# Flamingo block, batch 16: all issue offsets redone, q of the next batch between the score steps, values and sums apart, the last batch transposed by TensorE

## The chip, the cores and the metric

The kernel runs on 1 core of one Trainium2 chip. The metric is the device time of one execution in microseconds (us). A core has a matrix engine (TensorE, PE in the profile), VectorE (DVE), ScalarE (ACT), GpSimd (POOL) and a queue engine that issues DMAs (SyncE, SP). ACT and POOL can issue DMAs too. Each engine takes its own instructions strictly in order and waits on semaphores for the others.

## What is computed

Sixteen batches of x (512 rows of 512) pass a gated cross attention to 120 context rows of 384, and then a gated linear layer with int8 weights, whose input is quantised row by row. Reduced to what matters:

```python
q = split_heads(layernorm(x) @ Wq + bq)          # 16 heads of 32
k = split_heads(ctx @ Wk + bk)                   # 120 keys
v = split_heads(ctx @ Wv + bv)
out = softmax(q @ k.T / sqrt(32)) @ v
x = x + tanh(g_xattn) * (merge_heads(out) @ Wo + bo)
h = layernorm(x)
h_scale = max(absmax(h, row), 1e-6) / 127
h_q = round(h / h_scale)                         # int8
x = x + tanh(g_ffn) * ((h_q @ weight_q.T) * h_scale * weight_scale + bias)
```

## The kernel before

Work is done batch by batch. Each batch has five plans of small steps: A (first layer norm, split of x into a high and a low fp16 half, transposes), K (keys and values), Q (queries), D (scores, exps, values, division) and W (output projection, residual, second layer norm, quantisation, linear layer, store). A product of two fp32 matrices is made of three fp16 products (high by high, high by low, low by high), which is why q takes 12 matmuls for each of its four blocks.

There is no scheduler at run time. Each step is given to `at`, which looks up an offset in the table ORDER: by the step's name and arguments, and by which batch it is (the first four and the last two have a value of their own, the ten in the middle share one). The offset is added to 43.0 times the batch's number, all steps are sorted by that sum, and issued in that order. The offsets set only the order in which each engine gets its instructions; the time follows from the waits. Steps of up to four batches are in flight: in the middle of the run the loads of batch b+3, the layer norm of b+2, the q of b+1 and the scores of b lie between each other.

The steps that the text speaks of, with the engine and the line of the profile:

- `consts`, `mx`, `mxy`, `statq`, `scaleq` (the set-up S): maxima of the weights and of the context, from which powers of two for scaling (`s_q` among them) are made; lines 660 to 850. `w_q` is split only when `s_q` is known (L740 ACT, L747 DVE).
- A: `stats` (DVE, L981), `norm` and `high` (ACT, L997, L1004), `low` (POOL, L1009), `addb` (L1012, a DMA that POOL issues and that adds the row `bob` to x), `tr` (two DMA transposes by SP, L1022, into `xT`). In batch 0 TensorE transposes instead: `tp` (L1028) and `te` (ACT or DVE).
- K: `ld` and `tr` (SP, L1062 and L1074, into the single buffer `yT`), `kproj` (PE `pk`, 36 matmuls, L1098), `vproj` (PE `pvv`, 9, L1126).
- Q: `proj(j)` (PE `pq`, 12 matmuls of 128x512, L1158) for the four blocks j, `high` (ACT, L1168) and `low` (DVE `ql`, L1173); `mx(j)` (PE `pm`, 16 small matmuls on 32 rows each, L1182) and `red` (DVE, two maxima of 1.15 us, L1189); then `mh` (ACT, L1193), `mt` (PE `pmt`, L1200), `me` (ACT, L1204). `pmt` comes once a batch and marks its beginning here.
- D: `sc(j)` (PE `pss`, 16 matmuls on 32 rows, L1232), two `ex` (ACT, L1238), `av(j)` (values, PE `od<-P,V`, L1246) and `den(j)` (sums of the exps, PE `od<-P,sel`, L1253), both on 32 columns of the array, `ev` (ACT, L1261), `rec` (DVE, L1266), `shuf` (DVE, L1272), `mul` (POOL, L1277), `high` (ACT, L1282), `low` (POOL, L1285). In the last batch each is done in two halves of the columns.
- W: `wo` (PE `pw`, 48 matmuls, L1321), `res` (DVE, L1327), `st2`, `neg`, `cen`, `mxa` (the second layer norm and the row maxima), `addb` (L1351, a DMA by POOL that adds `fbb`; in the last batch `addf`, POOL, L1354), `scal1` to `scal3`, `quant` and `integ` (ACT, in the last batch DVE, L1382), `tr` (DMA transpose by SP into `xqT`, L1390), `ffn` (PE `pf`, 16 matmuls, L1398), `deq` (DVE `t`, L1403), `fin` (POOL, L1410, in the last batch DVE), `store` (SP, L1419), and in the last batch `warm` (PE, L1415).

Buffers that tie the steps: the scores and `pm` share two buffers of two banks (`ps_s`); `pq`, `pk`, `pvv`, `pmt` and `pf` share two buffers of one bank (`ps_g`); values, sums and `pw` share one buffer of two banks (`ps_o`, tile `od`; in the last batch `pw` uses `ps_s`); x has four buffers, so the load of a batch waits for the store of the one four before.

Of the kernel before, what the change touches and what calls it, by code (L numbers as in the profile page):

```python
# [36 lines left out]
        (): 20.285,  # L37
    },
    "S.constf": {
        (): -61.498,  # L40
    },
    "S.consts": {
        (): -65.108,
    },
    "S.consts1": {
        (): -64.857,
    },
    "S.consts2": {
        (): -34.332,
    },  # L50
    "S.consts3": {
        (): -26.254,
    },
    "S.copyb": {
        (): -60.711,
    },
    "S.down": {
        ('q',): -36.441,
        ('k',): -21.893,
        ('v',): -8.99,  # L60
    },
    "S.gate": {
        (): -3.985,
    },
    "S.gated": {
        ('bo', 0): 2.913,
        ('ws', 1): 0.661,
        ('fb', 1): 25.539,
    },
    "S.hi": {  # L70
        ('q', 0): -33.832,
        ('q', 1): -34.046,
        ('k', 0): -16.961,
        ('k', 1): -12.421,
        ('v', 0): -3.664,
        ('v', 1): -3.521,
        ('o', 0): -2.556,
        ('o', 1): 4.164,
    },
    "S.ld": {  # L80
        ('q', 0): -200.327,
        ('q', 1): -222.024,
        ('k', 0): -39.801,
        ('k', 1): -51.704,
        ('v', 0): -17.89,
        ('v', 1): -65.179,
    },
    "S.ldb": {
        (0,): -227.564,
        (1,): -210.907,  # L90
        (2,): -196.824,
    },
    "S.ldf": {
        (): -13.35,
    },
    "S.ldg": {
        (0,): -110.502,
        (1,): -17.854,
    },
    "S.ldo": {  # L100
        (0,): -56.994,
        (1,): -110.753,
    },
    "S.ldrow": {
        ('bv',): -32.795,
        ('bo',): -20.106,
        ('fb',): -109.216,
        ('ws',): -66.859,
    },
    "S.ldy": {  # L110
        (0,): -111.074,
        (1,): -200.113,
        (2,): -113.255,
        (3,): -67.61,
        (4,): -111.682,
        (5,): -111.646,
    },
    "S.lo": {
        ('q', 0): -33.546,
        ('q', 1): -33.653,  # L120
        ('k', 0): -11.456,
        ('k', 1): -11.206,
        ('v', 0): -2.02,
        ('v', 1): 1.162,
        ('o', 0): 24.181,
        ('o', 1): 23.573,
    },
    "S.mx": {
        ('q', 0): -195.144,
        ('q', 1): -191.105,  # L130
        ('k', 0): -33.438,
        ('k', 1): -26.29,
        ('v', 0): -16.889,
        ('v', 1): -18.355,
        ('o', 0): -19.212,
        ('o', 1): -23.931,
    },
    "S.mxy": {
        (0,): -33.367,
        (1,): -53.098,  # L140
        (2,): -33.403,
        (3,): -26.325,
        (4,): -31.401,
        (5,): -34.475,
    },
    "S.scalek": {
        (): -20.142,
    },
    "S.scalek2": {
        (): -19.177,  # L150
    },
    "S.scaleq": {
        (): -35.369,
    },
    "S.scalev": {
        (): -6.38,
    },
    "S.scalev2": {
        (): 3.092,
    },  # L160
    "S.scl_w": {
        ('v', 0): -5.773,
        ('v', 1): -5.165,
        ('o', 0): -3.771,
        ('o', 1): -3.592,
        ('k', 0): -19.963,
        ('k', 1): -12.707,
    },
    "S.spread": {
        ('q',): -36.227,  # L170
        ('k',): -21.607,
        ('v',): -6.881,
    },
    "S.statk": {
        (): -25.468,
    },
    "S.statq": {
        (): -58.209,
    },
    "S.statv": {  # L180
        (): -14.816,
    },
    "S.top": {
        ('q',): -45.163,
        ('k',): -22.858,
        ('v',): -10.92,
    },
    "S.trf": {
        (): 50.739,
    },  # L190
    "S.turnb": {
        (): -61.104,
    },
    "S.up": {
        ('q',): -46.128,
        ('k',): -23.895,
        ('v',): -12.6,
    },
    "S.warm": {
        (0,): -49.559,  # L200
        (1,): -28.506,
        (2,): -20.428,
        (3,): -35.19,
        (4,): -7.631,
        (5,): -43.983,
        (6,): -46.378,
        (7,): -36.405,
    },
    "load_x": {
        (): (-230.531, -172.483, -57.423, -63.392, -61.247, -83.98, -103.532),  # L210
    },
    "A.addb": {
        (): (16.961, 0.697, 2.556, -13.815, -39.944, -32.402, -15.602),
    },
    "A.high": {
        (0,): (-45.627, -67.038, -41.981, -38.764, -42.625, -39.408, -66.394),
        (1,): (-51.596, -71.041, -37.513, -38.693, -37.978, -50.31, -47.093),
        (2,): (-51.525, -71.077, -39.372, -38.729, -37.942, -50.202, -47.45),
        (3,): (-54.17, -66.43, -40.23, -38.657, -37.906, -38.228, -48.701),
    },  # L220
    "A.low": {
        (0,): (-41.445, -61.283, -40.552, -37.621, -30.257, -35.404, -52.311),
        (1,): (-48.844, -70.183, -32.152, -35.154, -37.656, -42.589, -44.162),
        (2,): (-40.266, -70.684, -37.263, -37.192, -37.335, -39.05, -30.079),
        (3,): (-50.167, -60.926, -39.086, -33.153, -31.115, -35.869, -31.33),
    },
    "A.norm": {
        (0,): (-60.747, -70.934, -43.518, -46.485, -43.447, -58.888, -67.86),
        (1,): (-51.632, -73.829, -42.053, -45.413, -43.876, -52.419, -60.246),
        (2,): (-59.925, -73.758, -41.731, -47.307, -44.555, -58.995, -48.558),  # L230
        (3,): (-55.957, -67.467, -41.052, -47.271, -43.375, -60.497, -66.609),
    },
    "A.scal1": {
        (): (-62.248, -76.617, -44.734, -55.85, -46.092, -70.576, -75.438),
    },
    "A.scal2": {
        (): (-61.069, -76.51, -44.591, -49.952, -45.448, -68.789, -74.901),
    },
    "A.stats": {
        (0,): (-207.118, -80.835, -52.883, -58.567, -49.202, -78.69, -75.902),  # L240
        (1,): (-204.259, -79.155, -52.562, -58.495, -53.741, -78.941, -86.697),
        (2,): (-203.651, -80.585, -52.74, -58.173, -56.636, -78.762, -80.478),
        (3,): (-204.009, -79.191, -54.063, -58.352, -55.385, -78.905, -83.123),
    },
    "A.te": {
        (0, 0): (-30.936, None, None, None, None, None, None),
        (0, 1): (-34.725, None, None, None, None, None, None),
        (0, 2): (-33.796, None, None, None, None, None, None),
        (0, 3): (-34.261, None, None, None, None, None, None),
        (1, 0): (-33.867, None, None, None, None, None, None),  # L250
        (1, 1): (-35.047, None, None, None, None, None, None),
        (1, 2): (-30.901, None, None, None, None, None, None),
        (1, 3): (-36.691, None, None, None, None, None, None),
    },
    "A.tp": {
        (0, 0): (-33.939, None, None, None, None, None, None),
        (0, 1): (-39.3, None, None, None, None, None, None),
        (0, 2): (-34.082, None, None, None, None, None, None),
        (0, 3): (-35.44, None, None, None, None, None, None),
        (1, 0): (-34.153, None, None, None, None, None, None),  # L260
        (1, 1): (-35.798, None, None, None, None, None, None),
        (1, 2): (-34.01, None, None, None, None, None, None),
        (1, 3): (-36.727, None, None, None, None, None, None),
    },
    "A.tr": {
        (0,): (None, -60.783, -28.399, -25.039, -25.754, -30.293, -21.75),
        (1,): (None, -56.601, -25.11, -32.044, -27.469, -31.866, -20.07),
    },
    "D.av": {
        (0, 0): (7.167, 6.702, 13.386, 9.025, -1.984, -0.161, 3.521),  # L270
        (1, 0): (8.775, 8.418, 16.782, 13.493, -1.233, 3.557, 6.881),
        (2, 0): (14.566, 9.776, 24.002, 14.744, 0.34, 20.07, 20.463),
        (3, 0): (20.642, 13.064, 26.147, 15.888, 5.558, 24.574, 25.897),
# [1222 lines left out]
```

## Time and profile before

| | us |
|---|---|
| median of 3 runs | 758.23 (757.19 to 759.46) |
| the profiled execution | 756.32 |
| its span, from the first to the last instruction | 754.5 |
| first `pmt` (batch 0) | 63.10 |
| last `pmt` (batch 15) | 695.47 |
| a batch from `pmt` to `pmt`, eight times in the middle | 42.73 |

In a profile, times of instructions are durations on the engine; matmuls overlap, so the time from the start of one to the start of the next tells more than a duration. A bracket after an instruction gives the idle time of its engine before it and what ended it. Rows with an x and a number merge that many instructions. The busy shares are PE 95%, DVE 75%, ACT 67% and POOL 60%; the clock granted to TensorE is full but for the very end.

### The profile page before, as it was taken

To read this page: it belongs to the slowest core of one execution; us is meant where nothing else is said; L and a number is where in the kernel's file an instruction comes from. 1 tells how busy PE (TensorE), PEld (TensorE's weight loads), DVE (VectorE), ACT (ScalarE), POOL (GpSimd) and SP (SyncE) were. 2 spreads that over 40 slices of the span, in tenths; PEclk is the share of its full clock that TensorE was granted. 3 is DMA by queue.
4 is the path that set the end of the run, shared out by engine and by line. 5 is a ranking of instruction groups with operands and counts; after the bars stand their busy time and mean duration, and the time that the engine had idled before them with its cause. 6 is when DMAs were issued, how large, how long until landed. Compare 5 with 4: busy or idle time off the path is not lost. (4 is left out here: it accounts for less than half of the span.)

```text
span 754.5 us, 15917 instructions
## 1 busy us (share of the span) xinstructions
PE 714.1 (95%) x6442; PEld 320.8 (43%) x6442; DVE 563.8 (75%) x1130; ACT 509.3 (67%) x742; POOL 450.0 (60%) x569
## 2 busy tenths in 40 slices
PE   4889899999999999999999999999999899999994
PEld 2344444444444444444444444444444344444441
DVE  5976767588686877869596877869596876768685
ACT  3657686675857686685858587685858566666850
POOL 5423856565765676656575776656565763665374
PEclk9999999999999999999999999999999999999997
DMA  9652575475897587784949688694949668565064
GB/s 346 186 142 77 96 115 102 89 193 93 191 135 169 107 172 157 99 211 76 210 73 199 120 148 180 96 205 76 207 85 177 152 113 195 93 144 84 2 139 140
DMA packets 137625, 105.55 MB, mean 140 GB/s; under 512 B 111691, under 2 KB 114135, under 8 KB 133583
## 3 DMA queue, kind: packets, MB, share of 16 engines
q1 hardware_dynamic: 120767, 71.24, 39.5%
q0 software_dynamic: 16368, 32.51, 25.8%
q8 instruction: 50, 0.82, 0.4%
q10 hardware_dynamic: 416, 0.79, 0.3%
q14 instruction: 24, 0.20, 0.1%
HBM read 27.65 MB, written 16.78 MB: 59 GB/s over the span
## 5 line engine op out<-in xcount | busy, mean ns | idle before, releaser
L1158 PE MATMUL pq<-xT,w_q 128*128 128x512 f16 x768 | 175.9, 382 | 6.3 <-DVE ql L1173 2.5
L1321 PE MATMUL pw<-w_o,ohl 128*128 128x512 f16 x768 | 176.7, 379 | 2.6 <-DVE x L1327 1.4
L1189 DVE TENSOR_REDUCE M<-pm 128x8 f32<-128x960 f32 x128 | 142.9, 1149 | 17.5 <-PE pm L1182 16.4
L1238 ACT ACTIVATE P<-pss,e_s 120x1024 f32<-120x1024 f32 (+1 forms) x136 | 137.4, 1061 | 25.0 <-PE pss L1232 24.5
L1158 PEld LDWEIGHTS <-w_q 128*128 128x128 f16 x768 | 72.5, 98 | 97.7 <-issue 12.7
L1321 PEld LDWEIGHTS <-ohl 128*128 128x128 f16 x768 | 72.2, 98 | 91.3 <-issue 6.7
L1009 POOL TENSOR_TENSOR xl<-xf,xh 128x512 f16<-128x512 f32 x64 | 77.2, 1280 | 55.3 <-ACT xh L1004 55.3
L1277 POOL TENSOR_TENSOR ou<-ou,R 128x512 f32<-128x512 f32 x60 | 75.5, 1270 | 50.8 <-DVE R L1272 50.1
L1410 POOL TENSOR_TENSOR x<-t,x 128x512 f32<-128x512 f32 x60 | 76.1, 1280 | 15.1 <-DVE t L1403 7.9
L1285 POOL TENSOR_TENSOR ohl<-ou,ohl 128x512 f16<-128x512 f32 (+1 forms) x68 | 73.5, 1099 | 10.9 <-ACT ohl L1282 10.9
L1403 DVE SCALAR_TENSOR_TENSOR t<-pf,xs,wsb 128x512 f32<-128x512 f32 x64 | 47.3, 741 | 42.2 <-PE pf L1398 40.9
L997 ACT ACTIVATE xf<-x,m,r 128x512 f32<-128x512 f32 x62 | 47.1, 802 | 45.8 <-DVE m L991 45.8
L1246 PE MATMUL od<-P,V 120*32 120x512 f32 (+1 forms) x544 | 69.0, 579 | 2.6 <-DVE x L1327 1.2
L1398 PE MATMUL pf<-w_f,xqT 128*128 128x512 f16 x256 | 67.1, 389 | 3.5 <-DMA xqT<-xq 3.5
L1253 PE MATMUL od<-P,sel 120*32 120x256 f32 (+1 forms) x1088 | 70.2, 371 | 0.0
L1168 ACT ACTIVATE qh<-pq,bq 128x512 f16<-128x512 f32 x64 | 43.7, 683 | 34.0 <-PE pq L1158 33.5
L1261 ACT ACTIVATE ou<-od,s_o 128x512 f32<-128x512 f32 (+1 forms) x68 | 45.1, 663 | 26.7 <-DVE rc L1266 14.4
L1282 ACT ACTIVATE ohl<-ou 128x512 f16<-128x512 f32 (+1 forms) x68 | 39.7, 600 | 31.6 <-POOL ou L1277 30.6
L660 DVE TENSOR_REDUCE am<-xc 128x1 f32<-128x512 f32 x64 | 42.1, 675 | 24.1 <-ACT xc L1345 24.1
L1253 PEld LDWEIGHTS od<-P,sel 120*32 120x32 f32 x1088 | 40.6, 109 | 44.5 <-issue 37.1
L1327 DVE SCALAR_TENSOR_TENSOR x<-pw,c_o,x 128x1024 f32<-128x1024 f32 (+1 forms) x34 | 41.3, 1217 | 23.9 <-PE pw L1321 23.9
L1173 DVE SCALAR_TENSOR_TENSOR ql<-pq,bq,qh 128x512 f16<-128x512 f32 x64 | 47.4, 740 | 12.3 <-ACT qh L1168 12.3
(151 smaller groups left out, 1049.7 us busy)
## 6 DMA issues: line engine op xcount, KB each, us to landing
x<-in_x_dram SPq DMA_DIRECT2D x16, 1024.0 KB, 5.1
x<-bob POOLq DMA_DIRECT2D x16, 1024.0 KB, 8.8
x<-fbb POOLq DMA_DIRECT2D x15, 1024.0 KB, 8.6
out_dram<-x SPq DMA_DIRECT2D x15, 1024.0 KB, 3.9
ys<-in_ctx_dram SPq DMA_DIRECT2D x6, 480.0 KB, 6.9
yt<-in_ctx_dram SPq DMA_DIRECT2D x16, 180.0 KB, 4.4
wfq<-in_L_xattn_Wq_dram SPq DMA_DIRECT2D x2, 512.0 KB, 5.9
wfo<-in_L_xattn_Wo_dram SPq DMA_DIRECT2D x2, 512.0 KB, 6.4
```

The lines of the kernel that those rows point to most:

```text
L1009: pool.tensor_tensor(box["xl"][:, s, :], box["xf", s], box["xh"][:, s, :], ALU.subtract)
L1158: pe.matmul(pq.rearrange("p (s t) -> p s t", t=128), w_q[:, wi, c, 128 * j : 128 * j + 128], xT[b, xi][:, c], start=n == 0, stop=n == 3 * ...
L1173: dve.scalar_tensor_tensor(QL[b][:, j, :], box["p", j], bq4[:, j : j + 1], QH[b][:, j, :], ALU.add, ALU.subtract)
L1189: dve.tensor_reduce(box["M"][:, 2 * h : 2 * h + 2, :, j], pm, AX.X, ALU.max)
L1238: act.activation(P[j, h, c], box["s", j, c][h][0:KV], AF.Exp, scale=e_s[0:KV])
L1246: pe.matmul(box["o", c][r], V[b][:, 128 * j + 32 * g : 128 * j + 32 * g + 32], P[j, g // 2, c][:, g % 2, :], start=True, stop=True, tile_p ...
L1253: pe.matmul(box["den", c][r, 0 : wd // 2], sel[:, h, j, :], P[j, g // 2, c][:, g % 2, wd // 2 * h : wd // 2 * (h + 1)], start=j == 0 and h ...
L1277: eng.tensor_tensor(u, u, box["R", g, c], ALU.mult)
L1285: pool.tensor_tensor(OT[b][:, 1, g, cols[c]], box["u", g][:, cols[c]], OT[b][:, 0, g, cols[c]], ALU.subtract)
L1321: pe.matmul(box["w", p][:, k, :], OT[b][:, oi, g, 128 * s : 128 * s + 128], w_o[:, wi, g, :], start=g == 0 and n == 0, stop=g == NG - 1 an ...
L1398: pe.matmul(pf.rearrange("p (o n) -> p o n", n=128), box["T"][:, s * CQ + c, :], w_fv[:, c], start=c == 0, stop=c == CQ - 1)
L1410: eng.tensor_tensor(x1, box["t", s], x1, ALU.add)
```

## The change

All values of ORDER are new. In the middle batches this does the following to the lists of the engines. On PE, q of the next batch, which stood in one piece after the last sums, begins before the last score step; 24 of the 48 `pw` of a batch go between the first and the second score step; `pk` follows the second score step; the sums of the third and fourth group go together, ahead of the values of those groups; `pf` goes to the end of the batch, just before `pmt`. On SP the store stands between the two transposes of x. In the set-up, all loads and maxima have another order; before the first `pmt` PE has one block of q of batch 1, where it had all four.

Beside ORDER three places change: two of the four `addf` of the last batch go to DVE; the odd `fin` of the batch before the last go to DVE; and the last batch's quantised rows are transposed by TensorE, with a copy by ACT, instead of by DMA. The core of the diff:

```diff
 ORDER = {
...
     "D.av": {
-        (0, 0): (7.167, 6.702, 13.386, 9.025, -1.984, -0.161, 3.521),
-        (1, 0): (8.775, 8.418, 16.782, 13.493, -1.233, 3.557, 6.881),
-        (2, 0): (14.566, 9.776, 24.002, 14.744, 0.34, 20.07, 20.463),
-        (3, 0): (20.642, 13.064, 26.147, 15.888, 5.558, 24.574, 25.897),
+        (0, 0): (1.782, -2.024, 0.467, 4.134, -1.574, 1.228, 2.024),
+        (1, 0): (3.096, 0.294, 5.691, 8.216, -0.778, 10.638, 7.317),
+        (2, 0): (19.424, 5.379, 13.509, 12.54, 1.193, 18.179, 10.741),
+        (3, 0): (25.34, 7.628, 22.019, 22.226, 2.508, 25.409, 23.922),
...
     "D.den": {
-        (0, 0): (7.172, 6.707, 13.391, 9.03, -1.979, -0.156, 3.526),
-        (1, 0): (8.78, 8.423, 16.787, 13.498, -1.228, 3.562, 6.886),
-        (2, 0): (14.571, 9.781, 24.007, 14.749, 0.345, 20.075, 20.468),
-        (3, 0): (20.647, 13.069, 26.152, 15.893, 5.563, 24.579, 25.902),
+        (0, 0): (1.816, -1.193, 0.502, 4.549, -1.228, 5.241, 2.473),
+        (1, 0): (2.992, 0.986, 6.659, 7.939, -0.917, 11.433, 7.109),
+        (2, 0): (17.21, 5.656, 13.232, 8.147, 0.225, 14.893, 10.015),
+        (3, 0): (19.217, 6.556, 13.301, 12.298, 2.439, 16.449, 16.968),
...
     "Q.proj": {
-        (0,): (-28.363, -55.814, -14.78, -23.752, -24.431, -28.22, -17.139),
-        (1,): (-24.109, -47.915, -13.1, -16.532, -24.145, -26.397, -16.818),
-        (2,): (-25.36, -46.7, -10.205, -12.635, -22.215, -21.107, -14.709),
-        (3,): (-20.821, -43.554, -5.451, -16.174, -17.568, -21.679, -12.493),
+        (0,): (-31.601, -42.291, -35.165, -37.655, -39.143, -61.317, -43.329),
+        (1,): (-10.638, -48.518, -24.302, -28.765, -36.79, -34.922, -35.787),
+        (2,): (-15.481, -37.932, -23.16, -22.261, -18.733, -34.611, -18.767),
+        (3,): (-9.323, -35.095, -18.525, -20.67, -29.56, -30.667, -23.922),
...
         def addf(s):
-            pool.tensor_tensor(xt[b][:, s, :], xt[b][:, s, :], fbb, ALU.add)
+            (pool if s < 2 else dve).tensor_tensor(xt[b][:, s, :], xt[b][:, s, :], fbb, ALU.add)
...
+        def trp(s):
+            if box.get("T") is None:
+                box["T"] = hp.tile([128, NS * CQ, 128], HP, tag="xqT", name="xqT")
+            box["tp", s] = pt = ps_s.tile([128, 2, 512], FP, tag="s", name="ptq")[:, 0, :]
+            for c in range(CQ):
+                pe.matmul(pt[:, 128 * c : 128 * c + 128], box["q"][:, s, 128 * c : 128 * c + 128], ident,
+                          start=True, stop=True)
+
+        def tre(s):
+            dst = box["T"][:, CQ * s : CQ * s + CQ, :].rearrange("d c p -> d (c p)")
+            act.activation(dst, box["tp", s], AF.Copy)
...
         def fin(s):
             x1 = xt[b][:, s, :]
-            eng = dve if last else pool
+            eng = dve if last or b == B - 2 and s % 2 else pool
             eng.tensor_tensor(x1, box["t", s], x1, ALU.add)
...
         if last:
             for s in range(NS):
                 at(2 * z + 48.5 + s, addf, s)
+                at(2 * z + 52.2 + 0.6 * s, trp, s)
+                at(2 * z + 52.5 + 0.6 * s, tre, s)
         else:
             at(2 * z + 48.5, addb)
...
-            at(2 * z + 52.2 + 0.6 * k, tr, k)
+            if not last:
+                at(2 * z + 52.2 + 0.6 * k, tr, k)
```

The seven values of a row are for batch 0, batch 1, the middle ones (4 to 13), batch 14, batch 15, batch 2 and batch 3. The first number that a call hands to `at` is not used; the offset comes from ORDER.

## The prediction

> **What bounds the kernel now.** The page's first part comes first, then TensorE's timeline over one batch.
>
> ```profile
> PE 714.1 (95%) x6442; PEld 320.8 (43%) x6442; DVE 563.8 (75%) x1130; ACT 509.3 (67%) x742; POOL 450.0 (60%) x569
> ```
>
> TensorE is the only engine near full, so an in-order engine that hardly waits sets the time. A batch period runs from one transposed-maxima step `pmt` (L1200) to the next:
>
> ```profile
> 395.45 0.40 PE L1200 MATMUL pmt<-ident,Mh 128*128 128x128 f16 x4
> 397.76 2.06 PE L1098 MATMUL pk<-yT,w_k 128*128 128x120 f16 x36
> 399.76 0.67 PE L1232 MATMUL pss<-qh,KHP 32*128 32x512 f16 x4
> ...
> 401.01 1.04 PE L1398 MATMUL pf<-w_f,xqT 128*128 128x512 f16 x4
> 401.97 1.07 PE L1246 MATMUL od<-P,V 120*32 120x512 f32 x8
> 402.86 1.08 PE L1253 MATMUL od<-P,sel 120*32 120x256 f32 x16
> 403.87 0.39 PE L1232 MATMUL pss<-qh,KHP 32*128 32x512 f16 x4
> ...
> 423.19 2.76 PE L1321 MATMUL pw<-w_o,ohl 128*128 128x512 f16 x12
> 425.79 2.75 PE L1158 MATMUL pq<-xT,w_q 128*128 128x512 f16 x12
> 428.38 2.75 PE L1321 MATMUL pw<-w_o,ohl 128*128 128x512 f16 x12
> 431.06 0.39 PE L1182 MATMUL pm<-KHP,qh 32*128 32x120 f16 x16
> 431.38 1.04 PE L1398 MATMUL pf<-w_f,xqT 128*128 128x512 f16 x4
> 432.50 2.75 PE L1321 MATMUL pw<-w_o,ohl 128*128 128x512 f16 x12
> ...
> 438.18 0.40 PE L1200 MATMUL pmt<-ident,Mh 128*128 128x128 f16 x4
> ```
>
> Read starts, not durations, which overlap. The period is 438.18 - 395.45 = 42.73. Twelve wide matmuls take 425.79 - 423.19 = 2.60, so 0.2165 each; before `pm` they take 2.68. `od<-P,V` takes 0.89, `od<-P,sel`, with the same work, 1.01. So each change between full, row-tiled and column-tiled matmuls costs 0.08 to 0.15. Two waits hide inside the durations: the second score step lasts 401.01 - 399.76 = 1.25 where the others last 0.98 (it waits for two exps of 1.06), and `pf` at 431.38 takes 1.12 for 0.87 (the next `pw` waits for the residual add). That is 0.27 + 0.25 = 0.52 a batch.
>
> The two ends are less tight. The start (timeline), then the end (windows, DVE and SP timelines):
>
> ```profile
> 40.83 1.02 PE L1158 MATMUL pq<-xT,w_q 128*128 128x512 f16 x4 [1.69 <-DMA xT<-xh]
> 43.18 3.56 PE L1158 MATMUL pq<-xT,w_q 128*128 128x512 f16 x8 [1.33 <-DMA xT<-xl]
> 63.10 0.38 PE L1200 MATMUL pmt<-ident,Mh 128*128 128x128 f16 x4 [0.98 <-DVE ql L1173]
> ```
>
> ```profile
> 738.20 2.61 SPq L1390 DMA_TRANSPOSE xqT<-xq  x2
> 742.70 4.45 PE L1398 MATMUL pf<-w_f,xqT 128*128 128x512 f16 x12 [0.15 <-DMA xqT<-xq]
> 747.93 2.49 DVE L1410 TENSOR_TENSOR x<-t,x 128x512 f32<-128x512 f32 x4
> ```
>
> The reader is to see q of batch 1 queued behind DMA transposes, and at the end a DMA transpose, then matmuls at 0.37 each, then DVE.
>
> **Sum by stages.** I priced TensorE's list of both programs by these spacings, with 0.09 to 0.15 per change of shape. Everything comes to 688.7 before and 688.3 after: the change moves work and removes none. The span of 754.5 is that work plus 65.8 of waits; only they can shrink.
>
> *Start to the first pmt.* Before: 38.8 of work, 63.1 of time, so 24.3 of waits. After, 36 of batch 1's q matmuls (7.8) stand behind this point: 31.0 of work. The q weights are ready later (DVE's list puts statistics of batch 1 and five maxima of 1.14 ahead of s_q: about 29 by the durations, 20.7 before), but `pk` no longer queues behind transposes. I keep 24.3: 55.3. Bounds: all of the later s_q shows (+8), or the two transpose waits and half the delay of `pk` go (-5).
>
> *First period.* Before 31.87 with 24.3 of work, 7.5 of waits (2.6 of them `pk` waiting for `yT`). After, 31.7 of work with q blocks between score steps, where the gaps were. Half the waits remain: 35.5; bounds 32.5 to 39.2.
>
> *Next three.* Before 129.6 with 126.0 of work; after 122.8 of work; the same waits: 126.4; bounds 124 to 130.
>
> *Eight steady periods.* After's batch is pmt, pf4, score 0, pw24, score 1, pk, values 0, sums 0, score 2, values 1, sums 1, pq12, score 3, pvv, sums 2 and 3, values 2, pm, pq24, pm, values 3, pq12, pm, pw12, pf8, pm, pf4, pw12. It has 20 changes of shape for 21 (-0.10). Both waits go: score 1 stands 5.2 behind score 0 (two exps need 2.1), score 2 4.9 behind score 1, and the second `pw` has pmt, pf4 and score 0 (2.3) for a residual add of 1.2. So 42.73 - 0.62 = 42.1. Cover by DVE rows, from pmt = 0: maxima (1.07 each) of block 2 end at -4.7, of block 3 at -1.0, `Mh` at -0.7; pmt needs it at 0. The first block's maxima end at 28.3, and `pm` of the next block needs their buffer at 29.4: 1.1 of cover. Cover that is gone costs one for one in each batch. On SP the store (3.9) now stands between `xT<-xh`, issued 1.7 past pmt, and `xT<-xl`, which lands 5.3 after its issue: between 10.6 and 17.7, read by pq12 at 16.2. I take the early end, as no accumulate runs then; the far end costs 1.5 a batch. Eight periods: 336.8; bounds 336 to 341.8 (no gain).
>
> *Sums apart from values.* Sums 3 end at 22.8 and values 3 at 30.7, so the reciprocal (1.76) and shuffles (0.35 each) run beneath pq24, and POOL multiplies three groups (1.27) and takes two lows (1.10) before the last values come; the last low ends at 37.2, its `pw` starts at 39.3. What is late next: values 3 needs `ev` of group 2, which waits for the reciprocal (as ACT does in before's waits, 14.4 in 11 times); it is there by 25.7.
>
> [...]
>
> *Last three periods.* Before 129.1 with 122.0 of work; after 125.3 plus 1.1 of the small losses that the steady period keeps and 1.6 of waits: 128; bounds 126 to 132.
>
> *Tail from the last pmt.* Before 59.0: 32.9 to the last `pw`, 22.0 to DVE's last add, 4.1 to the end. After, three `pf` leave the score steps, which then go by ACT at about 1.9 each (701.53 to 703.25 is 1.7): 34. Then SP's transposes, 738.20 to landing at 742.7, are replaced by 16 matmuls of 128 columns (four take 0.38 in the `pmt` row, 0.1 each) and four ACT copies (0.60, L1036). DVE becomes the bound: residual 0.75, statistics 0.87, four `xq` 2.5, two maxima 1.3, eight `t` of 0.74, scalars 0.75, and, taken over from POOL (1.28 there, 0.6 here), two odd adds of batch 14 and two addf, with four last adds 4.8: 16.9. With 0.25 of start and 4.1: 55.2; bounds 52 (DVE done earlier with batch 14's four `t`) to 59.
>
> Row first: matmuls of the last ten us ran at a granted clock of 0.67, 0.37 each. The sum takes the last 16 `pf` at 0.22, as DVE is behind them anyway; at the row's 0.37 they cost 2.4 more, inside the bounds above. [...]
>
> Sum: 55.3 + 35.5 + 126.4 + 336.8 + 128 + 55.2 = 737.2, where the span was 754.5. The profiled execution took 756.3, 1.8 more than its span, and the median of the runs is 1.9 above that: 737.2 + 3.7 = 741.
>
> **Rivals.** *Reorder without effect:* the work is equal (688.3), so if each stage keeps its waits, the total is 754 + 3.7 = 758. Against it: the two steady waits have visible causes. Half of it, the late s_q and no gain in the first period (+8, +4), gives 753.
>
> *Slower: transposes under POOL's accumulating DMA.* Before, SP's `xT<-xh` issue takes 6.6 to 6.84, ending as the bob accumulate (8.8) does:
>
> ```profile
> xT<-xh SPq DMA_TRANSPOSE x15, 8.2
> x<-bob POOLq DMA_DIRECT2D x16, 1024.0 KB, 8.8
> ```
>
> After, bob is issued some 20.6 past pmt, and on SP `yT`, held until `pvv` ends at 21.1, and `xqT` stand in its way. Bob ends at 29.4, `xqT` is issued then and lands 4.3 later, 33.7; `pf8` wants it at 36.3. The point is a bob of 11.4: the largest row is 12.6, and fbb, issued 7.6 before it, reaches 16.8. At 12.6 the loss is 1.2 a batch, 13 over eleven: 754; at 13.0 it is above before; at 14.5, 3.1 a batch, 775. For it: the two accumulates overlap by a microsecond. Against it: medians 8.6 and 8.8.
>
> *More than forecast:* the start's waits shrink too: 730.
>
> **How the numbers follow.** Forecast (733 to 749) 0.63; more 0.08; half the gain lost (749 to 755.9) 0.13; without effect 0.05; slower 0.11. A measurement of this kernel tells 0.3% (2.3 us) from no change: faster 0.84, same 0.05, slower 0.11. The range leaves out the tail beyond 757 and most of "more".
>
> **What would show it.** Right: pmt to pmt 42.1 in the middle; first pmt near 55; no DMA transpose before the last `pf`; DVE without gaps after the last `pw`. Wrong: TensorE waiting for `xqT` or `M` in every batch (second rival, or my 1.1 of cover), a first pmt above 60, or the last matmuls at 0.37 on the path.

## The result, and the profile after

The changed kernel took 760.9 us (median of 13 runs, 759.62 to 764.24), the kernel before 758.36 beside it (13 runs, 754.56 to 760.68). The ratio is 1.0039, with a 95% interval of 1.0023 to 1.0055: slower by 0.4%, where 741 us and a gain were forecast. The profiled execution of the changed kernel took 759.62, its span is 757.8. These are the busy times and the granted clock in 40 slices on its page:

```profile
PE 708.1 (93%) x6458; PEld 321.8 (42%) x6458; DVE 569.2 (75%) x1134; ACT 508.9 (67%) x746; POOL 450.5 (59%) x565
PEclk7699999999989999999999999999999999999999
```

TensorE still is the only engine near full, but its share has fallen. The steps from one `pmt` to the next tell where (us, from the timeline of TensorE; the stretch from the last `pmt` to the end is called the tail below):

| stretch | before | forecast | after |
|---|---|---|---|
| start to the first `pmt` | 63.1 | 55.3 | 64.5 |
| first period | 31.9 | 35.5 | 35.1 |
| next three | 129.6 | 126.4 | 135.2 (46.63, 38.81, 49.71) |
| eight steady | 341.8 | 336.8 | 334.8 (41.84 each, one 41.95) |
| last three | 129.1 | 128 | 126.0 |
| last `pmt` to the end | 59.0 | 55.2 | 62.3 |

The middle won more than forecast. Its rows in the timeline of the changed kernel (start, duration, engine, line, operation):

```profile
402.15 0.39 PE L1212 MATMUL pmt<-ident,Mh 128*128 128x128 f16 x4
402.37 1.03 PE L1423 MATMUL pf<-w_f,xqT 128*128 128x512 f16 x4
...
404.30 5.35 PE L1333 MATMUL pw<-w_o,ohl 128*128 128x512 f16 x24
409.59 0.39 PE L1244 MATMUL pss<-qh,KHP 32*128 32x512 f16 x4
...
410.56 2.06 PE L1110 MATMUL pk<-yT,w_k 128*128 128x120 f16 x36
...
440.52 1.04 PE L1423 MATMUL pf<-w_f,xqT 128*128 128x512 f16 x4
441.40 2.75 PE L1333 MATMUL pw<-w_o,ohl 128*128 128x512 f16 x12
443.99 0.39 PE L1212 MATMUL pmt<-ident,Mh 128*128 128x128 f16 x4
```

The reader is to see 443.99 - 402.15 = 41.84; score step 1 in 410.56 - 409.59 = 0.97 behind 5.3 us of `pw`, where it took 1.25; `pf` to the next `pw` in 0.88, where it took 1.12; and `pmt` to `pf` in 0.22. In the kernel before, where `pmt` began at 395.45, that last step took 0.37 (this row stands between the first two that the prediction shows):

```profile
395.82 1.04 PE L1398 MATMUL pf<-w_f,xqT 128*128 128x512 f16 x4
```

Before the first `pmt` and at the end the timeline of the changed kernel shows

```profile
38.50 2.75 PE L1170 MATMUL pq<-xT,w_q 128*128 128x512 f16 x12
...
64.47 0.38 PE L1212 MATMUL pmt<-ident,Mh 128*128 128x128 f16 x4 [1.76 <-DVE V L1145]
...
726.80 9.24 PE L1333 MATMUL pw<-w_o,ohl 128*128 128x512 f16 x42
...
747.35 3.82 PE L1423 MATMUL pf<-w_f,xqT 128*128 128x512 f16 x16
```

The first q matmul comes 14 us later than in the kernel before, the first `pmt` only 1.4 later. The last `pw` ends at 736.0, which is 40.5 after the last `pmt` (33.1 before), and from there to the end it is 21.8 (25.95 before). So the losses against the forecast lie in three places: the start (9.2), one period, that of batch 3 (49.71), and the score steps of the last batch (6.5).

### The profile page after: what moved, and what is told of

It reads as the page before. It is cut to its first block, busy times and chain, and to the rows that moved or that the text cites. A ratio compares the mean times of both kernels' runs of the same rounds, so it can differ in the third digit from the quotient of the medians.

```text
span 757.8 us, 15977 instructions
## 1 busy us (share of the span) xinstructions
PE 708.1 (93%) x6458; PEld 321.8 (42%) x6458; DVE 569.2 (75%) x1134; ACT 508.9 (67%) x746; POOL 450.5 (59%) x565
## 4 chain that ended last, share of the span: by engine, by line
PE 83%; DVE 6%; DMA 4%; ACT 4%; POOL 1%; issue 1%; SPq 0%; DVEq 0%; ACTq 0%; POOLq 0%
PE pw L1333 22%; PE pq L1170 20%; PE od L1265 8%; PE pss L1244 8%; PE od L1258 7%; PE pf L1423 7%; PE pk L1110 4%; PE pvv L1138 4%; PE pm L1194 2%; DMA x<-in_x_dram 2%; ACT P L1250 2%; DMA ys<-in_ctx_dram 1%; DMA wsb<-_L_ffn_weight_scale_dram 1%; DVE part L672 1%; POOL ou L1289 1%
## 5 line engine op out<-in xcount | busy, mean ns | idle before, releaser
L1021 POOL TENSOR_TENSOR xl<-xf,xh 128x512 f16<-128x512 f32 x64 | 75.0, 1178 | 22.8 <-ACT xh L1016 15.2
L1435 POOL TENSOR_TENSOR x<-t,x 128x512 f32<-128x512 f32 x58 | 74.0, 1288 | 18.6 <-DVE t L1428 18.4
L1339 DVE SCALAR_TENSOR_TENSOR x<-pw,c_o,x 128x1024 f32<-128x1024 f32 (+1 forms) x34 | 41.5, 1220 | 57.6 <-PE pw L1333 57.5
L1273 ACT ACTIVATE ou<-od,s_o 128x512 f32<-128x512 f32 (+1 forms) x68 | 44.9, 660 | 45.1 <-PE od L1265 18.1
L1357 ACT ACTIVATE xc<-x,nm 128x512 f32<-128x512 f32 x64 | 45.3, 716 | 29.2 <-POOL nm L1352 29.1
L1423 PE MATMUL pf<-w_f,xqT 128*128 128x512 f16 x256 | 63.2, 379 | 1.6 <-DVE t L1428 1.5
L1388 ACT ACTIVATE xc<-xc,magic,qs 128x512 f32<-128x512 f32 x64 | 50.2, 808 | 8.2 <-DVE qs L1380 8.2
L1265 PEld LDWEIGHTS od<-P,sel 120*32 120x32 f32 x1088 | 38.0, 111 | 41.3 <-issue 22.9
L1352 POOL TENSOR_SCALAR nm<-mv 128x2 f32<-128x2 f32 (+1 forms) x34 | 7.7, 225 | 77.4 <-DVE mv L1348 77.4
```

The costliest lines, as they stand in the source:

```text
L1021: pool.tensor_tensor(box["xl"][:, s, :], box["xf", s], box["xh"][:, s, :], ALU.subtract)
L1265: pe.matmul(box["den", c][r, 0 : wd // 2], sel[:, h, j, :], P[j, g // 2, c][:, g % 2, wd // 2 * h : wd // 2 * (h + 1)], start=j == 0 and h ...
L1423: pe.matmul(pf.rearrange("p (o n) -> p o n", n=128), box["T"][:, s * CQ + c, :], w_fv[:, c], start=c == 0, stop=c == CQ - 1)
L1435: eng.tensor_tensor(x1, box["t", s], x1, ALU.add)
```

## The experiments

Each ratio is to the kernel before in the same comparison; spans, periods and tails are those of the one profiled execution. Later experiments build on earlier ones, and the texts that were recorded ahead of them speak of them by number; the numbers stand in the headings and ahead of those texts.

### Batch 3: one pair of steps exchanged (experiment 1)

```
     "D.den": {
-        (2, 0): (17.21, 5.656, 13.232, 8.147, 0.225, 14.893, 10.015),
+        (2, 0): (17.21, 5.656, 13.232, 8.147, 0.225, 14.893, 10.086),
```

> One number of the changed kernel differs: in batch 3 the sums of group 2 (line 1265) are recorded just after the eviction of group 1 (line 1273) instead of just before it. No engine's list of instructions changes; only who waits for whom. Theory (values and sums lie in one PSUM tile, and what touches a tile is ordered as a whole, so this eviction waits for the sums although it reads only the values): ACT's wait of 6.26 us at 201.7 goes, the exps of the last score step come at about 205 instead of 211, and the period that took 49.71 us, which holds 4.8 of waits behind it and some 2.5 of matmuls at a lower clock, falls to 42.5 to 44; span about 751, 0.8% to 1.0% under the changed kernel. Rival (the period is long because the exps or the low part of k come late by themselves, from POOL or DVE): the period stays above 47 and the span within 2 us of 757.8.

Measured: 753.03 us, ratio 0.9968 (0.9950 to 0.9985), span 749.3; the period of batch 3 is 42.86, the other periods are unchanged, and the tail is 60.8 (62.3 in the changed kernel). ACT's timeline in the changed kernel:

```profile
199.60 2.11 ACT L1250 ACTIVATE P<-pss,e_s 120x1024 f32<-120x1024 f32 x2
207.97 0.69 ACT L1273 ACTIVATE ou<-od,s_o 128x512 f32<-128x512 f32 x1 [6.26 <-PE od L1265]
...
211.02 2.11 ACT L1250 ACTIVATE P<-pss,e_s 120x1024 f32<-120x1024 f32 x2
```

and in the experiment:

```profile
199.51 2.11 ACT L1250 ACTIVATE P<-pss,e_s 120x1024 f32<-120x1024 f32 x2
201.50 0.70 ACT L1273 ACTIVATE ou<-od,s_o 128x512 f32<-128x512 f32 x1
...
205.52 2.10 ACT L1250 ACTIVATE P<-pss,e_s 120x1024 f32<-120x1024 f32 x2
```

The eviction (L1273) needs values that were there at 201.1. It waited for the sums of the next group, which TensorE had behind q, a score step and `pvv`, and the exps of that score step stood behind it on ACT. With every engine's list unchanged, 6.85 us come back in that period.

### The last batch: sums behind their values (experiment 2)

```
-        (0, 0): (1.816, -1.193, 0.502, 4.549, -1.228, 5.241, 2.473),
-        (1, 0): (2.992, 0.986, 6.659, 7.939, -0.917, 11.433, 7.109),
...
+        (0, 0): (1.816, -1.193, 0.502, 4.549, -1.569, 5.241, 2.473),
+        (1, 0): (2.992, 0.986, 6.659, 7.939, -0.773, 11.433, 7.109),
...
```

> In the last batch alone every step of sums stands directly behind its step of values, as in the kernel before (for the last group the values are pulled ahead to the sums). Theory (the same tie of one tile: each eviction waits for the next group's sums, so that ACT's round trip is paid in every score step, and TensorE's waits then cost it its clock at 716 to 721): from the last pmt to the end of the last pw 34 to 36 us instead of 40.5, the tail 56 to 58 instead of 62.3, span 752 to 753. Rival (ACT sets these steps with 1.27 of exps, 0.47 of eviction and the four centrings, whatever the order): the stretch stays at 39 or more and the span within 2 us of 757.8.

Measured: 755.99 us, ratio 0.9993 (0.9974 to 1.0011), span 754.2. From the last `pmt` to the end of the last `pw` it is 34.8, the tail 56.7, as the theory had it; 1.7 of the gain went in the first period of this execution, where the first q block took 4.45 instead of 2.76. The time is that of the kernel before. From the last `pmt` to the last `pw` the granted clock was 1.00 (0.92 in the changed kernel). That the waits had cost the changed kernel its clock is not shown: in the last batch of the first experiment TensorE waited longer for evictions (3.8 and 1.8 us, against 2.6 and 1.8 in the changed kernel), with score rows of four at 0.11.

### The set-up in the old order (experiment 3)

The steps ahead of the first score step were sorted as in the kernel before, q of batch 1 apart; no code changed.

> The steps that the changed kernel records ahead of the first score step stand in the order of the kernel before; q of batch 1 stays between the score steps, and the statistics of batch 2, two of its normalisations and the load of batch 3 stand just behind or just ahead of the first score step. Theory (the first pmt is late since VectorE's list puts maxima that wait for loads ahead of the second normalised tile, the bias copy and s_q): s_q at about 20.7 instead of 31.5, first q matmul at about 24.5 instead of 38.5, first pmt at 56 to 59 instead of 64.5; span 750 to 753 if the first period keeps its 35. Rival (k's weights, v's chain and the eight maxima of the first batch set the first pmt, whatever stands ahead): first pmt at 62 or later, span within 2 us of 757.8, or what is won comes back in the first period.

Measured: 767.52 us, ratio 1.0158 (1.0122 to 1.0193), span 765.3. The first q matmul came at 24.26, as expected, and the first `pmt` at 66.46, later than in the changed kernel; the first period took 40.39. My edit had a fault of its own: I had put the load of batch 2 ahead of the transposes of batch 1, whose issue then took SP 8.9 us, so that `yt` of batch 1 was late and VectorE waited 5.69 for its high part ahead of k's bias. The granted clock, too, was only 0.55 to 0.76 between 40 and 66 us (1.00 from 40 to 60 in the changed kernel): `pk` took 3.78 (2.06 there), `pvv` 3.96 (2.10) and a q block 4.45 (2.76). So this run does not isolate the order; it shows that 14 us won on the first q matmul left no trace in the first `pmt`.

### The three together, and the first two (experiments 4 and 5)

Experiment 4:

> The three edits together. Theory: the three losses lie in different stretches and add up, so the span falls by 6.5 + 5.5 + 6.5 to about 739 and the time to about 742, which is what the prediction gave. Rivals: one of the stretches is paid back in the next (span 744 or more), or none of the three causes holds (span within 4 us of 757.8).

Measured: 754.28 us, ratio 0.9969 (0.9951 to 0.9988), span 753.1, not the 739 expected. The spans of the three do add up, but the start's part is a loss of 7.5, not a gain.

Experiment 5:

> The edits of the first two experiments together, the start as the change left it. Theory (two separate losses behind the tied tile): span 757.8 - 6.9 - 5.6 = 745 give or take the 2 us that the clock of the first 100 us moved between the runs so far, time about 749, 0.8% to 1.1% under the kernel before. Rival (the shorter tail and the shorter period share something): span above 748.

Measured: 748.54 us, ratio 0.9892 (0.9862 to 0.9922), span 746.6: the losses of batch 3 and of the tail are separate, and without them the change is faster than the kernel before.

### What the q work ahead of the first `pmt` cost (experiment 8)

In the kernel before, three q blocks of batch 1 with their evictions and low parts go behind score steps 0, 1 and 2 of batch 0. Other offsets shift with them, but nothing else changes its place in the list of an engine.

> The kernel before with one move: three of the four q blocks of batch 1 (36 wide matmuls, 7.8 us of work), their evictions and their low parts go from the stretch ahead of the first pmt to behind the first three score steps. The prediction's step (work taken away ahead of the first pmt shortens that stretch one for one): first pmt at 55 to 57 instead of 63.1, and the first period 3 to 5 longer. Rival (that work filled time in which TensorE would wait for k's weights and for the eight maxima of batch 0 on VectorE, which take 9 us and start at 51): first pmt at 59 to 62, and the first period 5 to 8 longer, so the span rises by 2 to 5.

Measured: 761.07 us, ratio 1.0060 (1.0035 to 1.0085), span 761.1. The first `pmt` comes at 62.32 instead of 63.10, the first period takes 38.72 instead of 31.87. The two largest waits of TensorE between 36 and 63 us in this experiment (in total, times, longest):

```profile
PE pm L1182 <- DVE M L1189: 4.2, 4, 1.3
PE pst L792 <- DVE stat L828: 3.2, 1, 3.2
```

and `pvv`, 2.12 in the kernel before, took 4.09 here, at a clock of 0.50. Of 7.8 us of work taken away 0.8 showed; the waits grew in its place, and the first period became 6.85 longer. The slower `pvv` had a part in this: `Mh`, which `pmt` needs, was there at 60.97, so with `pvv` at its 2.12 an estimated 2.1 at the most might have shown (63.10 - 60.97). Either way the prediction's step, at one for one, is refuted.

### The last batch by DMA transposes again (experiment 7)

```
-                at(2 * z + 52.2 + 0.6 * s, trp, s)
-                at(2 * z + 52.5 + 0.6 * s, tre, s)
...
-            if not last:
-                at(2 * z + 52.2 + 0.6 * k, tr, k)
+            at(2 * z + 52.2 + 0.6 * k, tr, k)
```

The two DMA transposes also get earlier offsets for the last batch.

> The fifth experiment with the last batch transposed by two DMA transposes in the places of the second and third group of TensorE's transposes, as in the kernel before. Theory (the transposes' part of the change is worth what the stretch from the last pw to the end says, 25.95 before and 21.8 after): span 3 to 5 above the fifth experiment. Rival (VectorE sets the end anyway): within 1 us of it.

Measured: 749.66 us, ratio 0.9904 (0.9869 to 0.9938), span 747.9; the tail 57.6 instead of 56.7. The transposes by TensorE are worth about 0.9, near the rival and far from the theory's 3 to 5: the last `pf` and VectorE's last add begin 0.5 later, VectorE's list behind the `pf` is the same, and the rest lies behind the last add.

### The adds back on POOL (experiment 10)

```
-            (pool if s < 2 else dve).tensor_tensor(xt[b][:, s, :], xt[b][:, s, :], fbb, ALU.add)
+            pool.tensor_tensor(xt[b][:, s, :], xt[b][:, s, :], fbb, ALU.add)
...
-            eng = dve if last or b == B - 2 and s % 2 else pool
+            eng = dve if last else pool
```

> The fifth experiment with the two odd last adds of batch 14 and the two adds of the bias of batch 15 back on POOL, as in the kernel before (0.68 and 0.6 to 1.0 each on VectorE, 1.28 to 1.5 on POOL). Theory (VectorE sets the end, as its list has no gap over 0.4 us in the last 20 us, and POOL is idle for 3.5 of them): last add 1 to 2.5 us earlier, span 744 to 745.5 against 746.6, with the same start. Rival (the end goes by the last pf matmuls, or POOL's slower adds take the place): within 0.5 of it or later.

Measured: 750.37 us, ratio 0.9913 (0.9878 to 0.9947), span 750.2, the tail 59.5 instead of 56.7. My theory fell: giving VectorE less to do made it later, by 2.8. VectorE's timeline

```profile
732.38 1.30 DVE L1394 TENSOR_SCALAR xq<-xc 128x512 f16<-128x512 f32 x1
733.60 1.22 DVE L1376 TENSOR_TENSOR a<-am,r 128x2 f32<-128x2 f32 x1
```

and POOL's in the same execution

```profile
732.12 1.28 POOL L1435 TENSOR_TENSOR x<-t,x 128x512 f32<-128x512 f32 x1
733.35 1.46 POOL L1366 TENSOR_TENSOR x<-x,fbb 128x512 f32<-128x512 f32 x1
```

show two VectorE instructions drawn out to the ends of two POOL adds (733.40 and 734.81) on the chain from the maxima to the quantised rows. In the fifth experiment they are

```profile
731.57 0.41 DVE L1394 TENSOR_SCALAR xq<-xc 128x512 f16<-128x512 f32 x1
731.91 0.15 DVE L1376 TENSOR_TENSOR a<-am,r 128x2 f32<-128x2 f32 x1
```

There POOL was idle beside them, from 731.38 to 734.93. So 2.0 of the 2.8 lie in these two; the rest comes behind them.

Each of the two ends within 0.3 us of the POOL add beside it (733.68 and 734.82 against 733.40 and 734.81). Why VectorE takes as long as POOL there, no run shows.

### The first four batches as in the kernel before (experiments 6, 9 and 11)

Everything up to the values' projection of batch 4 in the order of the kernel before, then the changed kernel's order with the first two edits. The place where the two orders meet is called the seam. Experiment 6:

> Everything that the kernel before records up to the values' projection of batch 4 stands in its order, the rest in the order of the changed kernel with both edits of the fifth experiment. Theory (the change is worth 0.9 us in each steady period and loses 3.2 in the first four batches even with batch 3 mended): fifth pmt at 224.5 instead of 227.7, then periods of 41.84, tail 56.7; span 742 to 744, time about 746, 1.2% to 1.6% under the kernel before. Rival (the periods of 41.84 need the order of the first four batches, or the seam costs a period): the period behind the seam is 45 or more and the span 746 or more.

Measured: 748.51 us, ratio 0.9888 (0.9855 to 0.9920), span 748.6. The periods ahead of the seam are 32.06, 42.21 and 43.00, the one behind it 49.70, then 41.84: the rival. VectorE waited 6.5 us there for the load of batch 5, with the low part of q behind, and the first `pmt` came at 64.17.

Experiment 9:

> The sixth experiment with its seam mended: VectorE's statistics of batch 5, which waited 6.5 us for a load with the low part of q of batch 4 behind them, stand behind the first maxima of batch 4. Theory (only that list order made the seam's period 49.7; the first four batches of the kernel before and the steady periods of the changed one fit together): period behind the seam 43 to 45, the others unchanged, span 742 to 744, time 743 to 746, 1.4% to 1.8% under the kernel before. Rival (the load of batch 5 itself is late by a store, so that its normalisation and transposes make q of batch 5 late): the loss comes back in the next period, 46 or more, and the span stays above 746.

Measured: 753.62 us, ratio 0.9957 (0.9936 to 0.9977), span 751.7. The period became 54.72: now the high part of q waited on ACT behind a normalisation of batch 5, and TensorE 9.6 for it. The theory of VectorE's list alone fell; the rival's loss in the next period did not come either, as that took 41.84.

Experiment 11:

> The sixth experiment with, instead of the ninth's edit, the last two final adds of batch 1, its store and the load of batch 5 (which takes that buffer) recorded some ten us earlier, right behind the last dequantisation of batch 1; VectorE's statistics of batch 5 stay where the sixth had them. Theory left by the ninth (the load of batch 5 itself came late, and all engines that the seam puts behind it): the statistics find their tile there, period behind the seam 43 to 46, span 742 to 745, time 743 to 747, below the fifth experiment. Rival (another step of the seam sets it, POOL's or ACT's): the period stays at 49 or more and the span above 746.

Measured: 751.81 us, ratio 0.9945 (0.9925 to 0.9966), span 751.7. The period was 53.80: the store moved ahead waited for its adds until 196.45, and the transpose of `xl`, now behind it on SP, made TensorE wait 8.82. The theory fell again; I left the seam there. Whether the old first four batches (3.2 us shorter) can be joined to the new middle stays open.

### Where the steady gain lies (experiment 12)

```
     "W.wo": {
-        (1, 0): (39.593, 21.708, 37.275, 37.24, 12.056, 38.243, 38.451),
+        (1, 0): (39.593, 21.708, 40.61, 37.24, 12.056, 38.243, 38.451),
...
     "K.kproj": {
-        (): (-22.192, -41.979, -43.432, -45.093, -49.14, -41.426, -45.577),
+        (): (-22.192, -41.979, -45.42, -45.093, -49.14, -41.426, -45.577),
```

> The fifth experiment with one block moved in the middle batches: the 24 wide output matmuls that stand between score steps 0 and 1 stand behind score step 1, and k's 36 narrow ones, which followed score step 1, stand between, as in the kernel before. TensorE's list alone changes, by place. Theory (what the steady period of 41.84 wins over 42.73 is cover: 5.3 us of matmuls hide the two exps of 1.06 between score steps, and k's 2.0 hide the residual add of 1.28 before the next values reuse the buffer): score step 1 waits 0.27 again, as in the kernel before, and values 0, which now stand right behind the output matmuls, wait about 1.5 for the add; periods 5 to 12 at 43.4 to 43.8, span 762 to 768. Rival (the order of these blocks does not matter and the 0.89 came from the fewer changes of shape or from ACT's and DVE's lists): periods within 0.3 of 41.84, span within 4 of 746.6.

Measured: 773.19 us, ratio 1.0219 (1.0183 to 1.0256), span 773.9, the periods 44.06. TensorE's timeline in one of them:

```profile
410.94 0.67 PE L1244 MATMUL pss<-qh,KHP 32*128 32x512 f16 x4
...
412.19 5.35 PE L1333 MATMUL pw<-w_o,ohl 128*128 128x512 f16 x24
418.92 1.07 PE L1258 MATMUL od<-P,V 120*32 120x512 f32 x8 [1.38 <-DVE x L1339]
...
422.29 1.06 PE L1258 MATMUL od<-P,V 120*32 120x512 f32 x8 [0.43 <-ACT ou L1273]
```

Score step 1 lasts 412.19 - 410.94 = 1.25 again, the values wait 1.38 for the residual add, as expected, and the next values 0.43 for an eviction, which I had not expected and which puts the period above the 43.4 to 43.8 of the theory. The same work in another place costs 2.2 us a batch. So the place of the block covers waits, and the 0.27 at score step 1 is shown to be one of them; the other two are new here. That the 0.25 at the second `pw` was cover too is read from the rows alone.

### A tile of their own for the last sums (experiments 13 and 14)

```
+                if last:
+                    box["den", c] = ps_g.tile([128, S], FP, tag="g", name="dn")[:, 0:wd]
```

Experiment 13:

> The first experiment (batch 3 mended), and in the last batch alone the sums lie in a PSUM tile of their own (a free buffer of the tag g) instead of in the second half of the tile of the values; every step keeps the place that the change gave it. Theory (it is the shared tile that makes evictions wait for the next sums and sums for the evictions, not their place in the order): TensorE no longer waits for the eviction ahead of the sums, the stretch from the last pmt to the end of the last pw falls from 40.5 to 34 to 36.5, as it did in the second experiment by order alone, tail 56 to 58.5, span 744.5 to 747.5. Rival (the order itself, sums of the next group ahead of the values, costs the time): the stretch stays at 39 or more and the tail above 60.

Measured: 747.11 us, ratio 0.9869 (0.9841 to 0.9896), span 744.2: the lowest median of all, though not clear of the noise below the fifth and the sixth, with the change's own order in the last batch. All waits of TensorE from the last `pmt` to 729 in this experiment:

```profile
PE pf L1425 <- DVE t L1430: 1.6, 1, 1.6
PE pss L1244 <- ACT P L1250: 1.0, 4, 0.3
PE od L1260 <- DVE x L1341: 0.8, 1, 0.8
PE dn L1267 <- ACT P L1250: 0.4, 1, 0.4
```

Not one for an eviction. In the same stretch of the first experiment, which differs only by the tile, they are

```profile
PE od L1265 <- ACT ou L1273: 3.8, 3, 1.4
PE od L1258 <- ACT ou L1273: 1.8, 3, 0.7
...
PE od L1258 <- DVE x L1339: 0.8, 1, 0.8
```

From the last `pmt` to the end of the last `pw` it is 33.9, against 39.1 there and 40.5 in the changed kernel. In the second and the fifth experiment, which keep the shared tile and change the order, it is 34.8. So it takes both, the shared tile and this order, to make the losses: a change of either one takes most of them away.

Experiment 14:

> The fifth experiment (batch 3 mended, sums directly behind values in the last batch) with the sums of the last batch in a PSUM tile of their own. Theory: of the waits that the fifth experiment keeps in the last score steps (0.36, 0.41 and 1.35 for an eviction) part goes, since the reciprocal and the evictions no longer order each other: tail 55 to 56.3 against 56.7, span 1 us below the fifth with the same start, time 746 to 748. Rival (ACT's exps and evictions, 1.74 a step, set these steps): tail 56.4 to 57, no difference.

Measured: 748.82 us, ratio 0.9891 (0.9869 to 0.9913), span 746.1, tail 56.5: no difference from the fifth experiment, the rival. With a tile of their own the sums seem to do better ahead of the values (tail 55.7) than behind, by 0.8 between one execution of each; the times (747.11 and 748.82) do not tell them apart.

## Why the prediction was wrong, step by step

Three steps failed: the start (by 9.2), the period of batch 3 (8.7) and the score steps of the last batch (6.5). The rest came out as forecast or better. The prediction gave "slower" a chance of 0.11, but for another cause, transposes under POOL's accumulating DMA, which did not come.

*Start to the first pmt ("I keep 24.3: 55.3").* This step failed, by 9.2. It took the waits as fixed and the work as what can go. The experiment with q moved shows the reverse: work that stood ahead of this `pmt` filled waits, and 0.8 of 7.8 came off (an estimated 2.1 at the most with `pvv` at its 2.12). The clock is not the cause: in the execution with the own tile TensorE had its full clock in the first 40 us (0.75 in the changed kernel's), with the first `pmt` at 64.49 against 64.47.

What sets it instead can be read from the traces, though no run isolates it. The first `pmt` follows the first high part of k (`KHP` on ACT) at a fixed distance: 13.26 in the kernel before and in the three experiments with its first four batches, 15.47 or 15.48 in the changed kernel and the eight with its start, 16.16 in the two with the old set-up and 13.56 in the one with q moved, where `pvv` took 4.09 at the lower clock. Between the two stand four rounds of `pm` with maxima of 2.2 us each, and `pvv`. In the changed kernel `pk` came 3.9 earlier than before, as forecast, but `KHP` only 0.8 earlier, as ACT's list has the scaling of `wsb`, which waits for its load, ahead of it. VectorE's, ACT's and again VectorE's timeline:

```profile
45.55 0.71 DVE L1119 SCALAR_TENSOR_TENSOR kf<-pk,c_k,bks 128x480 f32<-128x480 f32 x1
48.37 0.72 ACT L885 ACTIVATE wsb<-wsb,tg 128x512 f32<-128x512 f32 x1 [4.65 <-DMA wsb<-_L_ffn_weight_scale_dram]
49.00 0.59 ACT L1126 ACTIVATE KHP<-kf 128x480 f16<-128x480 f32 x1
59.50 1.81 DVE L879 TENSOR_TENSOR c_v<-pv,py 128x1 f32<-128x1 f32 x1
```

`KHP` could have begun at 46.26, 2.7 earlier; and `c_v`, ahead of the last two maxima, takes 0.15 in the third experiment and 1.81 here, to the end of a POOL instruction (61.28). By these rows an estimated 4.4 could go, to about 60, and 55.3 would still be missed.

*First period (35.5).* 35.06, right in the number; that half of the waits would stay was a guess, and the largest that stayed (2.08, values for the reciprocal) was not one that it named.

*Next three ("the same waits: 126.4").* Failed by 8.7. In the first two periods TensorE stood idle for 2.0 and 0.8; in the third, batch 3, for 4.7, and behind that it ran at a granted clock of 0.66 for ten us (211 to 221). The first experiment names the cause and takes 6.85 away. The prediction had read that values 3 wait for the eviction of group 2, and this for the reciprocal, and had not asked why an eviction of values should wait for the sums. That question held the answer: both lie in one tile of PSUM, what touches a tile goes in the recorded order, and a step that is recorded apart from its partner can order two engines that have nothing to say to each other.

*Eight steady periods (42.1).* The mechanism was right and the term too small: 41.84, and the eight together lie below its bounds. Of the gain of 0.89 the prediction's two waits and one change of shape are 0.62; `pmt` to `pf` (0.15) stood in the timeline before and was not counted; 0.12 are not assigned. Neither its 1.1 of cover for `pm` nor the second rival (transposes under POOL's accumulating DMA) decided anything: bob took 9.5 (median) and TensorE waits for no `xqT` there.

*Last three (128).* 126.0, at the lower bound: of the 2.7 that it added to the work 0.7 came.

*Tail ("which then go by ACT at about 1.9 each: 34", then 21.2).* The second part was right, 21.8. The first failed by 6.5: steps of 2.1 to 4.3 us, since evictions waited for the next sums and these for an eviction, and then the granted clock fell. With these waits and no such fall (first experiment) the stretch takes 39.1, and without the shared tile 33.9, the prediction's 34: 1.4 go with the clock, 5.2 with the tile. That VectorE nearly sets the end fits too, and hides most of what TensorE's transposes win: 0.9. What did pay there was what the sum had charged as a cost: the adds taken from POOL (2.8).

The sum of the steps with the two tied places mended is 64.5 + 35.0 + 128.3 + 334.7 + 126.0 + 55.7 = 744.2, the span of the own-tile experiment. Against the forecast's 737.2 that is 7.0 more: the start's 9.2 and 1.9 in the three periods behind the first, less 4.1 that the later periods won beyond it.

The last batch's waits for the eviction came from the program's tile, in this order, and not from the work: the own-tile experiment has the same values, sums and evictions in the same order, shows no wait for an eviction in that stretch, and is 5.2 us shorter there than the first experiment. What the two halves of one tile would need of each other without the recorded order, no run shows.

## What to carry to other kernels

Before steps are moved apart, look which of them touch the same tile: a tile that holds two results is a rope between engines, and a move that is free by the lists of each engine can pull on it (6.85 us in batch 3, 5.2 in the last batch); give each result its own tile, then order freely. Work ahead of a point shortens the way to it only if the engine does not wait there (0.8 of 7.8 us here): before you subtract, ask what arrives last at that point (here a part of k that stood behind a load of something else), and whether the work stood in a gap. And when an engine is relieved at a tight end, check what the one that takes over blocks (2.8 us here).

## What the runs showed of the chip

The granted clock fell without a long pause. In the changed kernel's last score steps TensorE never waited longer than 1.19 us at a time, and yet its clock was 0.50 from 717 to 723 us (0.68 on average from 713), with score rows of four at 0.18 to 0.22 where they had stood at 0.11 to 0.12. From 713 to 717, just ahead of the fall, it was busy for 2.11 of 4.0 us. In the first experiment the same matmuls came with the same waits (706 to 710, busy for 2.15) and the clock stayed at 1.00, the rows of four at 0.11, so the waits alone do not account for the fall. The kernel before, too, had less than the full clock ahead of its end: 0.84 from 45 to 50 us. What sets the clock, no run shows.

At the very end the prediction weighed 0.22 for each of the last 16 `pf` against the 0.37 of the kernel before's last ten us. They took 3.82 together in the changed kernel, at a granted clock of 1.00, near the 3.5 of 16 times 0.2165.

Three short VectorE instructions were drawn out beside a POOL instruction: 1.30 and 1.22 us in the tenth experiment, where they took 0.41 and 0.15 in the fifth with POOL idle, and 1.81 for `c_v` in the changed kernel, which took 0.15 in the third experiment. The first two cost 2.0 us at the end of that run. With one 1 MB load issued just ahead of it, the issue of a DMA transpose on SP took 8.9 us in the third experiment, where it had taken 4.4 in the changed kernel; whether the load alone made the difference was not tested.
